# A clearing of an unread tile behind each gather in a two-layer graph network

## The chip, the cores and the metric

The kernel runs on one core of one Trainium2 chip. A core has five engines that work side by side, each in its own order: TensorE (PE; its weight loads are shown as PEld), VectorE (DVE), ScalarE (ACT), GpSimd (POOL) and SyncE (SP). They wait for each other through semaphores. Data moves between HBM and the on-chip memory SBUF through 16 DMA engines. Most transfers are issued by SP. Gathers, which fetch rows by a list of indices, are issued by GpSimd[...]. The metric is the device time of one execution in microseconds.

## The reference, cut to what matters

There are N = 3327 nodes with D = 256 features and an adjacency matrix of 3327 x 3327 whose entries are nonzero with a chance of 0.0024, plus the diagonal. So a row of it has about 9 nonzero entries.

```
h = relu(layernorm(x))
Xf = Xa = h;  Z = 0
R = (adj + I) / rowsum(adj + I)
for n in 0, 1:
    A  = top_p_attention(Xa, W1, W2, W3)   # softmax rows, cut to the largest that hold 0.9
    Xf = R @ Xf
    Xa = A @ Xa
    Z += Xf @ U1[n].T + Xa @ U2[n].T
x = x + layernorm(h + Z) * ln_g + ln_b     # layer 0
h = relu(layernorm(x))
d = (rowsum(adj) + 1e-9) ** -0.5
out = x + relu((d * adj * d) @ h @ W.T + b)   # layer 1
```

The attention is dense in its logits (3327 x 3327). The products with R and with the scaled adjacency are sparse. All numbers are float32.

## The kernel before, in words

The nodes are cut into 26 blocks of 128 rows (`NB`). The work is in stages that overlap at their edges. A start normalizes the nodes and makes keys, queries and products with weights. In stage 1 each block of the first attention step (`block_0`) runs beside `listing`, which finds the nonzero blocks of the adjacency, and `products_0`, the first sparse product. In stage 2 each block of the second attention step (`block_1`) runs beside `products_1`, the second sparse product. The last stage is the sparse product of layer 1 with its output product: 10 blocks of it (`DENSE`) as dense products over all of the adjacency's columns (`dense_product`, L1636), 16 by gathered rows.

**A sparse product by gathers.** For 128 rows, `listing` makes 8 slots (`SLOTS`) of 128 indices each. `gather_adj` (L759) fetches for one slot 128 pieces of adjacency rows into the tile `ac`; 8 of them make a block, and the result is stored to HBM (`ac_hbm`) and loaded again where it is needed. `gather_node` (L773) fetches for one slot 128 rows of 256 values (of `gb_hbm` in stage 1, `y_hbm` in stage 2, `hn_hbm` in the last stage) into a tile `vg`. `adj_gathered` (L783) multiplies the two on TensorE and sums over the 8 slots. There are 16 tiles `vg`, handed round in a list (`nodes_free`): a gather into one waits until TensorE has read it for the product before. In all there are 208 gathers of `ac` and 208 + 208 + 128 of `vg`, 752 together; in stage 1 a block has 16, in stage 2 and in a gathered block of the last stage 8. GpSimd's only other regular work is one addition per block in stage 2 (`add_bet`, L1349).

**What else runs beside them.** An attention block has logits on TensorE (L947), exponentials (L964) and passes over the whole row on ScalarE (L1008), a window pass (`window`, L1130) and a pass that drops what isn't kept (`drop_rest`, L1195) on VectorE, with small sorting steps between, turns of the weights on TensorE (L1209), copies by ScalarE (L1215) and the sum over values (`attend_sum`, L1224). The window and drop passes read 128x3327 values through two inputs in SBUF.

**What sets the order.** The order is written out by hand-kept numbers. `PLACES` names every step of each kind of block with a time; `BASES`, `PERIODS` and `SHIFTS` place the blocks, `MOVED` has blocks of their own, `EVENTS` single steps. `Plan` sorts all steps by these numbers and issues them one after the other. Each engine then does its share of them in that order, as soon as its waits are over; the numbers set no times beyond that.

Of the kernel before, what the change touches and what calls it, by code (L numbers as in the profile page):

```python
# [55 lines left out]
CODE = 4096  # L56
OFFSET = 4000.0
# [48 lines left out]
BASES = (-1.219, 871.121, -13.308, 19.608, 850.942, -80.36, 1724.847, 1716.49)  # L106
PERIODS = (30.0457, 29.9102, 30.2729, 28.5772, 29.0439, 1.6, 11.4283, 31.0222)
# [11 lines left out]
        ldq=-54.13, lg0=-39.852, ex0=-35.489, lg1=-29.838, ex1=-21.663, guess0=-20.859, guess1=-19.422,  # L119
        guess2=-19.336, guess3=-18.872, guess4=-18.507, guess5=-18.37, guess6=-15.915, ev1r=-13.296, ev1s=-9.29,  # L120
        st10=-8.997, st11=-5.99, guess7=-4.744, guess8=-3.502, st12=-3.403, st13=-3.094, st14=-1.343, st15=-1.159,
        st16=-0.991, st17=0.794, st18=1.518, win=9.292, wm2=9.574, wm1=9.968, wm3=12.534, wm0=12.544, sort0=13.403,
        cut0=14.026, sort1=14.125, sort2=14.543, sort3=16.481, sort4=17.004, sort5=17.559, sort6=17.939,
        sort7=18.592, thr=18.602, sort8=20.105, sort9=20.115, cut1=22.238, cut2=22.369, cut3=23.418, cut4=23.885,
        cut5=25.085, drop=25.681, inv=29.153, tr0=30.66, atc0=31.107, tr2=33.099, atc2=33.099, cut6=34.08,
        tr1=36.246, att0=36.894, atc1=37.192, tr3=40.273, atc3=41.533, att1=41.65, tr5=43.272, att2=44.935,
        att3=45.175, atc5=46.936, tr4=47.048, atc4=47.748, tr6=48.232, att4=52.752, atc6=54.181, att5=54.906,
        att6=58.725, attend=59.33, xtk_t=61.309, xtk_c=61.351, k_m=63.572, k_c=64.152, q_c=64.162, xu_m=66.376,
        xu_c=67.443, stxt=67.497, edge=70.682, stxu=75.618, stq=110.443,
    ),  # L130
    dict(
        ldq=-84.641, lg0=-64.92, ex0=-46.665, lg1=-45.76, ex1=-42.611, guess0=-42.569, guess1=-42.249,
        guess2=-42.014, guess3=-40.793, guess4=-40.513, guess5=-40.41, guess6=-40.216, ev1r=-34.894, ev1s=-32.942,
        mass0=-31.704, mass1=-31.672, mass2=-28.358, tail0=-26.851, tail1=-26.741, tail2=-26.526, tail3=-25.436,
        st10=-25.416, st11=-24.309, half=-23.772, aux0=-23.184, st12=-22.188, ev2s=-22.046, st13=-19.038,
        aux2=-18.425, thr=-17.708, st14=-16.622, btw1=-16.127, aux1=-13.861, sec10=-9.799, sec11=-7.489, sec12=-5.93,
        sec13=-5.256, nt2=-2.764, win=6.431, wm3=8.61, wm2=9.266, wm1=9.617, wm0=9.627, sort0=10.242, sort1=10.835,
        sort2=11.685, sort3=11.777, cut0=11.935, sort4=11.985, sort5=13.173, sort6=14.573, sort7=16.994,
        sort8=17.581, sort9=18.189, cut1=18.77, cut2=20.296, cut3=22.388, cut4=24.395, cut5=25.055, match=26.793,
        drop=27.95, tr0=29.85, tr1=31.048, atc0=31.434, tr2=32.44, atc1=32.946, edge=33.058, inv=33.905, att0=34.774,  # L140
        att1=34.905, atc2=35.47, tr4=35.49, tr3=36.814, att2=37.708, atc3=38.537, tr6=38.857, atc4=39.087,
        tr5=40.433, att3=40.469, atc6=45.474, atc5=46.334, att4=47.311, att5=47.868, att6=48.525, ldh=55.755,
        resid0=58.172, resid1=59.911, resid2=65.149, ldx=66.891, input20=69.622, root1=70.415, xbet=71.254,
        input21=73.884, input22=77.99, input23=79.538, root2=80.212, node2=88.781, stn=116.191,
    ),
    dict(
        lda1=-111.852, lda0=-108.627, flag1=-106.679, lda2=-105.584, flag0=-103.568, lda3=-101.391, flag2=-91.791,
        flag3=-91.183, listA0=-90.203, listA1=-87.679, listA2=-86.532, listA3=-82.435, listA4=-81.321,
        listA5=-78.466, listA6=-77.573, listN=-77.097, listA7=-76.714, listA8=-74.027, before=-70.418,
        beforec=-69.957, owners0=-68.346, owners1=-67.51, owners2=-63.593, shared=-56.741, lentc=-55.686,  # L150
        rows0=-50.814, rows1=-50.724, rows2=-47.7, rows3=-47.197, rows4=-42.132, rows5=-41.699, rows6=-41.116,
        rows7=-40.982, ga2=-14.404, ga0=-9.852, ga3=-4.385, ga4=-3.687, ga5=-2.371, ga1=-1.471, ga6=-0.85,
        ga7=-0.422, store=6.48,
    ),
    dict(
        gv4=5.839, gv2=20.97, gv1=22.589, gv6=25.502, lda=34.921, gv5=39.836, gv3=42.6, gv0=50.085, adj0=53.225,
        adj1=54.857, gv7=55.367, adj2=57.006, ldg=57.925, adj3=58.421, adj4=60.115, adj5=60.458, adj6=64.105,
        adj7=65.535, prop=68.632, roots=69.135, mixy=79.312, stxf=80.78,
    ),
    dict(  # L160
        gv4=8.024, gv2=8.104, gv0=13.177, ldt=16.082, gv3=17.924, gv6=25.033, gv7=28.341, lda=28.341, gv1=28.38,
        gv5=28.405, mix0=31.627, ld2=32.167, adj0=32.509, adj1=32.918, adj2=33.108, adj3=33.284, adj4=33.367,
        adj5=33.829, adj6=34.626, adj7=35.6, prop=44.561, scale=48.985, resid0=50.228, sthz=58.643,
    ),
    dict(
        mom=-13.994, node=-0.02, turn=0.915, turnc=2.784, proj=4.77, qc=7.477, stq=8.657, kc=9.12, gb=9.864,
        gc=10.785, stg=12.8, sth=161.359,
    ),
    dict(
        load=-27.7, gath=-6.539, prod=6.899, m=11.709, turn=14.704, mt=15.242, ldx=18.62, out=22.03, add=23.58,  # L170
        st=32.732,
    ),
    dict(
        row=-138.454, first=-124.233, second=-66.949, m=-52.332, ldx=-43.509, turn=-31.128, mt=41.499, out=99.246,
        add=109.349, st=109.933,
# [5 lines left out]
        12.63, 15.58, 13.76, 9.52, 14.85, 12.16, 7.33, 10.92, 12.38, 9.62, 10.05, 9.11, 6.13, 3.87, 5.9, 4.83, 5.04,  # L181
        3.38, -0.12, -0.81, -1.16, 0.73, -0.82, -1.47, -2.43, -4.06,
    ),
    (
        -3.42, -2.88, -2.0, -4.0, -2.87, -3.95, -4.64, -4.98, -5.17, -5.79, -6.06, -7.02, -7.66, -7.46, -7.61, -7.57,
        -8.28, -7.59, -8.88, -8.46, -8.36, -8.16, -9.1, -8.01, -8.45, -5.21,
    ),
    (
        48.05, 45.26, 47.07, 44.35, 35.7, 41.0, 31.58, 32.35, 22.91, 21.61, 15.75, 22.72, 14.28, 11.86, 11.76, 7.75,
        16.82, 22.71, 18.19, 32.24, 28.12, 25.64, 29.93, 25.27, 39.31, 42.78,  # L190
    ),
    (
        1.89, 8.61, 12.55, 21.95, 15.88, 24.02, 9.78, 15.75, 7.52, 3.91, 1.26, 4.72, 27.1, 31.73, 24.74, 37.8, 36.46,
        33.98, 33.66, 26.09, 37.71, 39.86, 24.21, 40.27, 31.79, 24.39,
    ),
    (
        -0.19, 2.55, 4.61, 10.25, 4.67, 3.99, 4.78, 7.69, 5.45, 6.63, 18.14, 12.33, 6.62, 6.28, 18.49, 11.75, 18.86,
        15.25, 8.72, 17.78, 22.41, 20.1, 23.47, 16.81, 9.48, 50.95,
# [5 lines left out]
        ldq=-53.671, lg0=-40.889, ex0=-37.137, lg1=-36.052, ex1=-32.766, guess0=-32.08, guess1=-32.08,  # L204
        guess2=-26.639, guess3=-26.046, guess4=-23.558, guess5=-23.104, guess6=-19.495, ev1s=-19.05, ev1r=-16.237,
        st10=-14.643, st11=-9.001, st12=-8.515, st13=-7.998, guess7=-6.427, st14=-6.323, guess8=-2.775, st15=-1.334,
        thr=-0.993, st16=0.358, st17=0.452, st18=4.273, win=4.393, wm0=7.365, cut0=7.398, wm3=8.486, wm2=8.644,
        wm1=9.137, sort0=9.72, sort1=10.861, sort2=12.3, sort3=12.31, sort4=15.195, sort5=15.397, sort6=15.646,
        sort7=16.912, sort8=17.349, sort9=18.279, cut1=20.61, cut2=20.899, cut3=22.232, cut4=22.242, cut5=23.179,
        drop=23.189, tr1=24.549, atc1=26.309, tr0=27.037, tr6=27.22, atc0=28.666, tr3=32.131, att0=32.131,  # L210
        att1=32.207, atc6=33.868, tr2=34.238, atc2=35.068, att2=35.264, atc3=38.695, tr4=41.024, tr5=48.015,
        atc5=49.222, att3=50.742, atc4=50.911, att4=50.919, att5=51.122, inv=51.9, att6=56.244, attend=57.45,
        xtk_t=58.899, xtk_c=60.185, k_m=66.789, edge=67.629, q_c=68.534, k_c=72.714, xu_m=75.139, stxt=85.201,
        xu_c=87.454, stq=93.482, cut6=93.886, stxu=100.697,
    ),
    (0, 1): dict(
        ldq=-96.445, lg0=-49.921, ex0=-34.349, lg1=-32.938, ex1=-28.697, guess0=-25.972, guess1=-25.962,
# [91 lines left out]
        adj4=-5.716, adj5=5.842, adj6=12.279, adj7=23.93, prop=24.426, scale=30.347, resid0=39.4, sthz=45.469,  # L309
    ),  # L310
    (6, 1): dict(
        load=-130.829, gath=-4.41,
    ),
    (6, 2): dict(
        gath=-14.181, load=3.453,
# [1554 lines left out]
```

## Time and profile before

Three runs took 1693.52, 1696.96 and 1696.99 us.

| | |
|---|---|
| Time of the runs, median | 1696.96 us |
| Profiled execution, its own time | 1863.65 us |
| Its span in the profile | 1861.8 us |
| Mean granted clock of TensorE in it | 0.94 |
| Gathers of `ac`, L759 | 208, 265.4 us busy, mean 1276 ns |
| Gathers of `vg` from `gb_hbm`, L773 | 208, 244.3 us busy, mean 1175 ns |
| Gathers of `vg` from `y_hbm`, L773 | 208, 301.6 us busy, mean 1450 ns |
| Gathers of `vg` from `hn_hbm`, L773 | 128, 121.3 us busy, mean 948 ns |
| First and last start of a gather in stage 1 | 101.6 and 908.7 us |
| First and last start of a gather in the last stage | 1629.2 and 1832.0 us |

The profiled execution took 9.8% longer than the runs, so its durations are those of that execution. Idle time is put down to what ended it. "Issue" is time in which an engine waited for nothing that the profile shows. "Remote" or "another core or an unknown queue" is a wait whose end the profile can't name; on one core that is a transfer or an instruction without a record. Some of TensorE's records are missing.[...]

### The profile page before, as it was taken

Reading aid. Unit: us, or ns where it says so; the run is one execution under the profiler, and the core shown is the slowest. Engines: PE = TensorE matmul, PEld = TensorE weight load, DVE = VectorE, ACT = ScalarE, POOL = GpSimd, SP = SyncE. Lnnn points to the kernel's source line nnn. Section 1 sums busy time; section 2 is a strip of 40 time slices with the busy share of each in tenths; the row PEclk is TensorE's granted clock in tenths of the full one; section 3 lists DMA queues with packets and bytes.
Section 4 is the critical chain, followed back from the end, with each engine's and each line's share of the span. In section 5 each row is a group of like instructions: output and inputs, shape, how many; then the busy total and the mean of one; then the engine's idle time right before and its main releaser. Section 6 shows DMA issues by size and latency. Waiting matters only on the chain.

```text
span 1861.8 us, 25048 instructions
## 1 busy us (share of the span) xinstructions
PE 1555.0 (84%) x7444; PEld 1202.7 (65%) x7444; DVE 1316.8 (71%) x3963; ACT 1147.3 (62%) x2694; POOL 964.7 (52%) x792
## 2 busy tenths in 40 slices
PE   5947788697899888888848989999989988988887
PEld 3526566475677565666636767777767767777676
DVE  5488678676898876766278899999989999601112
ACT  3566476465778665654387989998979986200000
POOL 0067467665677555754345345454555553065652
PEclk9959789898999898989979999999999999999999
DMA  6556656555555544543533333333334334356752
GB/s 188 170 161 190 191 151 183 175 167 161 152 181 179 175 144 132 176 135 109 159 95 91 107 108 111 113 115 95 114 107 135 92 117 147 114 201 216 240 171 88
DMA packets 148400, 272.54 MB, mean 146 GB/s; under 512 B 29347, under 2 KB 94240, under 8 KB 146976
## 3 DMA queue, kind: packets, MB, share of 16 engines
q1 hardware_dynamic: 109456, 183.94, 30.5%
q0 software_dynamic: 32768, 84.98, 16.2%
q10 hardware_dynamic: 6032, 1.93, 0.4%
q8 instruction: 61, 1.00, 0.2%
q14 instruction: 83, 0.68, 0.1%
HBM read 221.34 MB, written 49.41 MB: 145 GB/s over the span
## 4 chain that ended last, share of the span: by engine, by line
PE 46%; ACT 21%; DVE 14%; issue 8%; another core or an unknown queue 7%; DMA 2%; ACTq 0%; SPq 0%; DVEq 0%
PE att_acc L1224 16%; ACT ja L1008 8%; PE adj_acc L783 6%; PE p_t L1209 5%; PE p_l L947 5%; PE late_sums L1636 4%; ACT e L964 4%; ACT at L1215 3%; DVE cand L1137 3%; PE p_gb L857 2%; DVE w L1190 2%; PE late_acc L783 2%; DVE e L1195 2%; PE p_turn L807 1%
## 5 line engine op out<-in xcount | busy, mean ns | idle before, releaser
L1008 ACT ACTIVATE ja<-e,t 128x3327 uint8<-128x3327 f32 x127 | 389.6, 3068 | 1.7
L773 POOL DMA_INDIRECT vg<-y_hbm,v_idx x208 | 301.6, 1450 | 171.1 <-PE adj_acc L783 79.5
L759 POOL DMA_INDIRECT ac<-in_adj_t,a_idx x208 | 265.4, 1276 | 209.4 <-DVE crowd L697 89.0
L1224 PE MATMUL att_acc<-h,at 128*128 128x256 f32 (+1 forms) x1352 | 337.5, 397 | 35.3 <-ACT at L1215 34.8
L773 POOL DMA_INDIRECT vg<-gb_hbm,v_idx x208 | 244.3, 1175 | 178.0 <-PE adj_acc L783 103.8
L1215 ACT COPY at<-p_t 128x512 f32<-128x512 f32 (+1 forms) x364 | 193.9, 546 | 230.3 <-remote 82.1
L1224 PE MATMUL att_acc<-xa,at 128*128 128x256 f32 (+1 forms) x1352 | 325.0, 389 | 11.9 <-ACT at L1215 8.4
L1224 PEld LDWEIGHTS att_acc<-h,at 128*128 128x128 f32 (+1 forms) x1352 | 262.5, 200 | 80.8 <-ACT at L1215 38.7
L1224 PEld LDWEIGHTS att_acc<-xa,at 128*128 128x128 f32 (+1 forms) x1352 | 256.1, 195 | 50.4 <-ACT at L1215 12.6
L1209 PE MATMUL p_t<-ident,e 128*128 128x128 f32 x1352 | 208.2, 285 | 89.5 <-ACT at L1215 30.5
L1209 PEld LDWEIGHTS p_t<-ident,e 128*128 128x128 f32 x1352 | 162.7, 146 | 146.5 <-ACT at L1215 40.8
L783 PE MATMUL adj_acc<-vg,ac 128*128 128x257 f32 (+1 forms) x832 | 228.4, 398 | 15.2 <-DMA vg<-y_hbm,v_idx 7.3
L1137 DVE MAX8 cand<-w 128x8 f32<-128x208 f32 x832 | 238.3, 360 | 0.9
L947 PE MATMUL p_l<-kt,q 64*128 64x512 f32 (+1 forms) x832 | 191.1, 576 | 39.3 <-ACT e L964 33.8
L1130 DVE SCALAR_TENSOR_TENSOR w<-e,t 128x3327 f32<-128x3327 f32 x52 | 191.3, 3678 | 12.7 <-ACT u L978 4.7
L783 PEld LDWEIGHTS adj_acc<-vg,ac 128*128 128x128 f32 x832 | 154.6, 197 | 47.0 <-issue 10.1
L964 ACT ACTIVATE e<-p_l 128x2048 f32<-128x2048 f32 x104 | 161.6, 1554 | 28.6 <-PE p_l L947 8.0
L773 POOL DMA_INDIRECT vg<-hn_hbm,v_idx x128 | 121.3, 948 | 90.2 <-PE late_acc L783 54.1
L947 PEld LDWEIGHTS p_l<-kt,q 64*128 64x128 f32 x832 | 77.1, 198 | 128.6 <-issue 80.8
L1349 POOL TENSOR_TENSOR x_in<-x_in,bet 128x256 f32<-128x256 f32 x26 | 30.1, 1159 | 208.9 <-DMA x_in<-in_x 169.7
L811 ACT COPY xt_k<-p_turn 128x256 f32<-128x256 f32 x52 | 19.3, 373 | 161.4 <-PE p_turn L807 69.4
L651 DVE TENSOR_REDUCE most<-adj_sb 128x7 f32<-128x896 f32 x104 | 104.2, 1012 | 17.7 <-DMA adj_sb<-in_adj_t 7.9
(397 smaller groups left out, 2219.2 us busy)
## 6 DMA issues: line engine op xcount, KB each, us to landing
adj_sb<-in_adj_t SPq DMA_DIRECT2D x78, 448.0 KB
ac<-ac_hbm SPq DMA_DIRECT2D x68, 512.0 KB
adj_row<-in_adj_t SPq DMA_DIRECT2D x10, 1664.0 KB
ac_hbm<-ac SPq DMA_DIRECT2D x26, 512.0 KB
adj_sb<-in_adj_t SPq DMA_DIRECT2D x26, 320.0 KB
gb_hbm<-gb SPq DMA_DIRECT2D x26, 256.0 KB
gb<-gb_hbm SPq DMA_DIRECT2D x26, 256.0 KB
q<-q_hbm SPq DMA_DIRECT2D x104, 32.0 KB
```

The costliest lines, as they stand in the source:

```text
L651: nc.vector.tensor_reduce(s["most"][:, b0 : b0 + nb], s["chunk"].pop(c)[:, :nb, :], AX.X, ALU.max, apply_absolute_value=True)
L759: nc.gpsimd.indirect_dma_start(s["list"][:, k, :], None, adj_rows, bass.IndirectOffsetOnAxis(ap=s["a_idx"][:, k : k + 1], axis=0))
L773: nc.gpsimd.indirect_dma_start(t[:, :D], None, hbm[:, :], bass.IndirectOffsetOnAxis(ap=v_idx[:, i, k : k + 1], axis=0))
L783: nc.tensor.matmul(s["acc"][:, :width], s["ac"][:, k, :], rows[:, :width], start=(k == 0), stop=(k == SLOTS - 1))
L947: nc.tensor.matmul(pl[:, at : at + cw], s["q"][rows, :], kt[rows, c0 + c : c0 + c + cw], start=True, stop=True)
L964: nc.scalar.activation(halves(s["e"])[:, :, c0 : c0 + w], logits_of(s.pop(("l", g)))[:, :, :w], AF.Exp, accum_out=s["zp"][:, g : g + 1],)
L1008: nc.scalar.activation(junk, s["e"][:, :N], f, bias=s["t"], scale=-1.0, accum_out=s[name])
L1130: nc.vector.scalar_tensor_tensor(w[:, :N], ev, s["t"], ev, op0=ALU.is_le, op1=ALU.mult, accum_out=s["below"])
L1137: nc.vector.max(s["cand"][:, 8 * n : 8 * n + 8], s["w"][:, c0 : c0 + cw])
L1209: nc.tensor.transpose(pt[:, c : c + P], s["e"][:, b * P : (b + 1) * P], ident)
L1215: nc.scalar.copy(at[:, :w], pt[:, :w])
L1224: nc.tensor.matmul(s["att"][:, :D], at[:kb, c : c + P], v[b][:kb, :D], start=(b == 0), stop=(b == NB - 1))
```

## The change

Behind each gather, in `gather_adj` and in `gather_node`, GpSimd clears a tile `pace` of 128 x 576 float32 values. Nothing reads that tile. `BASES`, `PERIODS`, `PLACES`, `SHIFTS`, `MOVED` and `EVENTS` have new numbers throughout, and so every engine's order is a new one. The program has the same instructions as before apart from the 752 clearings. The lines of the new file stand 1 to 11 further down.

```diff
+PACE = 576
...
-BASES = (-1.219, 871.121, -13.308, 19.608, 850.942, -80.36, 1724.847, 1716.49)
-PERIODS = (30.0457, 29.9102, 30.2729, 28.5772, 29.0439, 1.6, 11.4283, 31.0222)
+BASES = (-1.195, 870.965, -13.311, 19.642, 853.079, -80.36, 1724.577, 1718.463)
+PERIODS = (30.0441, 29.9154, 30.273, 28.5719, 28.9512, 1.6, 11.802, 30.9401)
...
-        ga7=-0.422, store=6.48,
+        ga7=-0.66, store=9.794,
...
-        gv4=5.839, gv2=20.97, gv1=22.589, gv6=25.502, lda=34.921, gv5=39.836, gv3=42.6, gv0=50.085, adj0=53.225,
-        adj1=54.857, gv7=55.367, adj2=57.006, ldg=57.925, adj3=58.421, adj4=60.115, adj5=60.458, adj6=64.105,
-        adj7=65.535, prop=68.632, roots=69.135, mixy=79.312, stxf=80.78,
+        gv4=5.632, gv2=20.714, gv1=22.346, gv6=25.618, gv5=40.164, gv3=42.721, lda=44.817, gv0=50.312, adj0=52.657,
+        ldg=53.654, adj1=53.856, gv7=55.447, adj2=55.715, adj3=57.708, adj4=59.865, adj5=63.091, adj6=63.222,
+        adj7=64.567, roots=65.776, prop=68.869, mixy=74.572, stxf=96.762,
...
-        load=-27.7, gath=-6.539, prod=6.899, m=11.709, turn=14.704, mt=15.242, ldx=18.62, out=22.03, add=23.58,
-        st=32.732,
+        load=-23.985, ldx=0.485, gath=6.212, prod=12.722, m=19.141, turn=23.257, mt=24.311, out=26.194, add=31.048,
+        st=35.891,
...
-    keys=-30.497, centre=773.083, nodes=801.366, hn=830.787, last_nodes=902.39, roots=904.614, hn_last=1508.035,
+    keys=-30.531, centre=763.84, nodes=824.78, last_nodes=899.443, hn=928.418, roots=969.659, hn_last=1378.645,
...
     node_space = const.tile([P, 2 * SLOTS, D + 1], F32, name="vg")
+    pace = const.tile([P, PACE], F32, name="pace")
+
+    def paced():
+
+        nc.gpsimd.memset(pace, 0.0)
+
...
         nc.gpsimd.indirect_dma_start(
             s["list"][:, k, :], None, adj_rows, bass.IndirectOffsetOnAxis(ap=s["a_idx"][:, k : k + 1], axis=0)
         )
+        paced()
...
         nc.gpsimd.indirect_dma_start(
             t[:, :D], None, hbm[:, :], bass.IndirectOffsetOnAxis(ap=v_idx[:, i, k : k + 1], axis=0)
         )
+        paced()
```

## The prediction

> **What bounds the kernel now.** I read first the page's shares, then the stretches of the three stages, then GpSimd's (POOL's) own timeline. The page's first part says that no engine is full on average:
>
> ```profile
> PE 1555.0 (84%) x7444; PEld 1202.7 (65%) x7444; DVE 1316.8 (71%) x3963; ACT 1147.3 (62%) x2694; POOL 964.7 (52%) x792
> ```
>
> The 52% understates POOL. The busy times by stretch, with the stages cut where the gathers start and end (columns: stretch; its length; busy us of PE, PE's weight loads, VectorE, ScalarE, POOL; TensorE clock; DMA share; GB/s), and below them four blocks of stage 1 that ran almost undisturbed:
>
> ```profile
> 101.00:911.00 810.00, 658.09 (x3179) 503.98 (x3176) 602.01 (x1937) 488.97 (x1213) 510.42 (x417) 0.91 0.53 161
> 950.00:1610.00 660.00, 585.95 (x2895) 459.94 (x2896) 616.28 (x1720) 564.46 (x1233) 330.29 (x232) 0.97 0.37 112
> 1629.00:1841.00 212.00, 184.56 (x833) 156.69 (x833) 27.61 (x66) 10.48 (x30) 121.32 (x128) 0.97 0.60 197
> ...
> 543.60:648.40 104.80, 92.22 (x464) 70.62 (x463) 89.13 (x288) 74.83 (x184) 70.33 (x55) 0.96 0.57 179
> ```
>
> Stage 1 is bound by PE with stalls, stage 2 by VectorE (93%), the last stage by PE. In stage 1 a block takes 30 us on average by the starts of its window pass (L1130), 26.2 in those four (543.6 to 648.4). POOL's timeline there shows what its busy time leaves out: 0.30 us before each gather, and long gathers:
>
> ```profile
> 510.42 0.94 POOL L759 DMA_INDIRECT ac<-in_adj_t,a_idx  x1 [0.30 <-issue]
> 511.67 3.22 POOL L759 DMA_INDIRECT ac<-in_adj_t,a_idx  x1 [0.30 <-issue]
> 515.20 0.94 POOL L759 DMA_INDIRECT ac<-in_adj_t,a_idx  x1 [0.30 <-issue]
> ```
>
> VectorE's timeline has the reason, the drop pass from 510.38 to 514.08; the long gather ends 0.8 us after it:
>
> ```profile
> 510.38 3.70 DVE L1195 SCALAR_TENSOR_TENSOR e<-e,kept 128x3327 f32<-128x3327 f32 x1
> ```
>
> So one gather costs POOL 0.945 + 0.30 = 1.245 us, and a window or drop pass (two per block) holds it up for about 2.7 us more. In the four blocks POOL is taken for 70.3 + 55 x 0.30 = 86.8 of 104.8 us: 4.5 us per block are free. And PE already waits for POOL at times. The chain of waits around 440 us:
>
> ```profile
> 440.04 0.47 ACT at L1215
> 440.51 10.07 another core or an unknown queue
> 450.58 0.57 ACT at L1215
> ```
>
> In these 10 us POOL ends a run of 14 gathers with nothing between them (430.45 to 447.6), and PE resumes at about 450: I read it as PE standing at a product of gathered rows (L783) until the last of them had landed, with everything behind it in PE's order, the turns that ScalarE waits for among it.
>
> [...]
>
> **The change part by part.** *The clearing.* One 128x576 memset behind each of 208 + 208 + 208 + 128 = 752 gathers. Its size is not in the trace; the two nearest rows are
>
> ```profile
> masks.py:197 POOL MEMSET ident<- 128x128 f32 x1 | 0.2, 204 | 0.3 <-POOLq L1859 0.3
> L1859 POOL MEMSET const-float32-0.0<- 128x1 f32 x1 | 0.1, 98 | 0.2 <-issue 0.2
> ```
>
> (204 - 98)/127 = 0.83 ns per element, so 98 + 575 x 0.83 = 0.58 us; with the other one-column rows (up to 118 ns) it is 0.51.[...] I take 0.55. The gaps come from the only other work between gathers, the add L1349:
>
> ```profile
> 966.34 4.21 POOL L773 DMA_INDIRECT vg<-y_hbm,v_idx  x1 [0.30 <-issue]
> 970.57 0.73 POOL L1349 TENSOR_TENSOR x_in<-x_in,bet 128x256 f32<-128x256 f32 x1
> 971.46 0.97 POOL L773 DMA_INDIRECT vg<-y_hbm,v_idx  x1 [0.16 <-issue]
> ```
>
> The add follows the gather after 0.02 us, the next gather the add after 0.16, and lasts 0.97. So a paced gather takes 0.02 + 0.55 + 0.15 + 0.97 = 1.69 us in place of 1.245: +0.44. Ends: +0.25 if clearing and gap overlap, +0.60 if the gap stays 0.30 and the clearing is 0.58. In all 752 x 0.44 = 331 us of POOL time. The clearing waits only for the clearing before it, long done; queued behind it is the next gather, and for that PE's product.
>
> *Stage 1.* 416 gathers x 1.69 = 703 us, plus holds: now 509.7 - 416 x 0.945 = 117 us; a denser POOL meets each of the 52 passes, 52 x (3.68 - 1.69/2) = 147. Demand 820 to 850 us in a stretch of 810 that now has 810 - 510 - 125 (gaps) = 175 us free. That free time doesn't go to zero, since POOL works in order and waits for freed row tiles (104 us on PE adj_acc) and indices (23 us); as PE then waits for POOL, these shrink. I keep a third, 58 us: 835 + 58 - 810 = +83 us.
>
> *Stage 2.* 8 gathers per block, 208 x 0.44 = 92 us, and 330 + 208 x 0.30 = 392 of 660 taken now: 484 of 660. VectorE at 93% covers it: 0. Uncovered, the eighth gather of a block is 3.5 us late, at most 15 us over the stage where PE stood on it.
>
> *Last stage.* First to last gather 1629.2 to 1832.0 = 203 us; 127 x 1.69 = 215: +12, and of the 44 us that it waits now (54 us on late_acc by the waits) some stays: +18.
>
> *The order.* Against the old order, no gather moves by more than one place among POOL's gathers. Stage 1's gathered products move on average 0.4 places earlier in PE's order, by at most 22; so they get no more lead. Only in the last stage are they 11 places later on average and dense products as much earlier, which the +18 (not +26) takes in. SP's stores of y come 5 places later, its loads of gb 3 earlier, in a queue that mostly waits for VectorE; VectorE's edge step and ScalarE's thr, some 0.2 us each, move most. I put all that at 0, at most 10 us either way: a moved step that is late stalls PE as at 440.
>
> Sum: 83 + 0 + 18 + 0 = 101 us on the profiled 1861.8 (1863.65 with what lies around it). The timed runs are 165 us shorter, by what the trace can't say. If all stages shrink alike, stage 1 is 740 us and a demand of 835 overruns it by more; if gathers themselves are quicker there, by less. I keep about +98: 1697 + 98 = 1795.
>
> **The rivals.** *Hidden.* In timed runs a gather is much cheaper than 1.245 us; at 0.9, stage 1 demands 416 x 1.34 + 147 = 705 of 740 and the last stage is free: about +15, 1712. For it: the missing 165 us, much of which is PE stalled on gathers. Against: the four good blocks had 4.5 us free and get 16 x 0.44 = 7.0. *Saturated.* Pitch as in the profile and a stage of 740: 835 + 58 - 740 = +153, last stage +26: 1876. *Faster.* The new order of the last stage: PE idles there 212 - 184.6 = 27 us, mostly at gathered rows that are late; with dense products first all of it could go: 1670. It decides only if stage 1's clearings are free, that is for a gather under 26.2/16 - 0.44 - 5.7/16 = 0.84 us. That spacing itself helps speaks against the trace: rows land no later after long runs of gathers than after lone ones (the medians are near 2 us in both). *Nothing.* The clearing can't be left out: it is an instruction of its own.
>
> **How the numbers follow.** Slower by the sum or towards saturation 0.66 (own range 1740 to 1885); hidden 0.16; faster 0.14; within 0.2%, about what a measurement can tell from no change, 0.04. So faster 0.14, same 0.04, slower 0.82. The range drops most of the faster case and the top of the saturated one: 1690 to 1880.
>
> **What would show it.** Clearings of 0.5 to 0.6 us; 0.15 us before the gather behind each; POOL over 85% taken in stage 1; PE's waits on an unknown queue longer, its clock below 0.91 there; stage 2 unchanged. Wrong if the gaps swallow the clearing, or if stage 1 keeps 30 us a block.

## The result, and the profile after

The changed kernel takes **1881.67 us** (median of four runs, 1879.86 to 1882.07). The kernel before takes 1696.97 us beside it. The ratio is 1.109, with an interval of 1.107 to 1.111: the change costs 185 us. The forecast was 1795 us, with a range of 1690 to 1880.

One fact is needed to read every number below. In the experiments the kernel before takes 1695 to 1697 us on two chips, one set of runs on each, and 1865 to 1869 us on two others, one of which was used twice. I call them chips I and chips II. That it is the chip, and not something else that differed from one set to the next, is not shown beyond these five sets. Chips I are compared with chips I and chips II with chips II, unless the text says otherwise. By its times the result is of chips I, and the profile ahead of the prediction, at 1864 us, of chips II. The first experiment, a repeat of the kernel before on a chip I, has the profile to lay beside the profile after.

The first part of the page, in the kernel before on a chip I, and after:

```profile
PE 1508.6 (89%) x7444; PEld 1178.1 (69%) x7444; DVE 1316.4 (78%) x3963; ACT 1145.9 (67%) x2694; POOL 995.1 (59%) x792
```

```profile
PE 1566.1 (83%) x7444; PEld 1205.4 (64%) x7444; DVE 1335.4 (71%) x3963; ACT 1141.7 (61%) x2694; POOL 1381.4 (73%) x1544
```

POOL went from 995 us to 1381 us of busy time. TensorE, at a granted clock of 0.93 in place of 0.97, went from 1509 to 1566; the other two kept theirs. POOL's row of the 40 slices (busy tenths) shows where, first in the kernel before on a chip I:

```profile
POOL 0047658888888868886273554355565653166762
```

and after:

```profile
POOL 0059999999999999899958855665865584289994
```

Stage 1 (slices 3 to 20) is 9 nearly throughout, and so is the last stage but for its ends. Stage 2 between them is not. By stretch (columns as in the prediction; the first stretch after ends 42 us past the last gather of stage 1), after:

```profile
101.00:1000.00 899.00, 698.80 (x3329) 534.56 (x3326) 653.55 (x2019) 536.57 (x1326) 795.86 (x854) 0.88 0.50 153
1000.00:1640.00 640.00, 593.24 (x2986) 466.80 (x2986) 600.87 (x1685) 548.54 (x1213) 390.00 (x427) 0.99 0.39 120
1640.00:1880.00 240.00, 200.17 (x852) 162.28 (x850) 32.42 (x78) 12.33 (x36) 193.62 (x251) 0.91 0.52 168
```

and the kernel before on a chip I:

```profile
102.00:798.00 696.00, 626.51 (x3194) 490.17 (x3192) 600.50 (x1935) 488.17 (x1214) 536.22 (x416) 0.96 0.61 187
798.00:1493.00 695.00, 618.07 (x3073) 482.80 (x3070) 632.97 (x1755) 596.17 (x1311) 335.49 (x236) 0.97 0.39 118
1493.00:1698.00 205.00, 190.11 (x889) 162.36 (x887) 32.37 (x78) 12.62 (x36) 121.45 (x128) 0.99 0.63 208
```

TensorE's clock fell from 0.96 to 0.88 in stage 1 (0.89 over its gathers alone, 107 to 958 us) and from 0.99 to 0.91 in the last stage, the two in which it now idles longer: 177 of 851 us over those gathers in place of 69 of 696, and 40 of 240 in place of 15 of 205. Whether the idle time lowers the clock was not tested. Two groups of the page, in the kernel before on a chip I (busy us, mean ns, idle us before it and what ended most of that):

```profile
L773 POOL DMA_INDIRECT vg<-gb_hbm,v_idx x208 | 278.5, 1339 | 78.1 <-issue 42.2
L783 PE MATMUL adj_acc<-vg,ac 128*128 128x257 f32 (+1 forms) x832 | 222.7, 390 | 9.3 <-DMA vg<-y_hbm,v_idx 6.7
```

and after:

```profile
L631 POOL MEMSET pace<- 128x576 f32 x752 | 447.6, 595 | 0.4
L768 POOL DMA_INDIRECT ac<-in_adj_t,a_idx x208 | 274.5, 1320 | 130.4 <-DVE a_idx L757 96.4
L794 PE MATMUL adj_acc<-vg,ac 128*128 128x257 f32 (+1 forms) x832 | 229.0, 402 | 88.5 <-DMA vg<-gb_hbm,v_idx 43.8
L783 POOL DMA_INDIRECT vg<-gb_hbm,v_idx x208 | 255.9, 1230 | 38.5 <-issue 27.8
```

A clearing takes 595 ns and waits for nothing (0.4 us ahead of all 752). The idle time ahead of the gathers from `gb_hbm` was 78 us, of which 23 us came from waiting for row tiles that TensorE still had to read. Now 38.5 us are left, mostly the gap that each has, and the waits for row tiles are 1 us. The dependence has turned round: TensorE stands 88.5 us ahead of L794, half of it for rows of `gb_hbm`, where it stood 9 us ahead of L783 and not for those. POOL's timeline in stage 1:

```profile
498.93 2.95 POOL L768 DMA_INDIRECT ac<-in_adj_t,a_idx  x1 [0.17 <-issue]
501.88 0.60 POOL L631 MEMSET pace<- 128x576 f32 x1
502.64 0.95 POOL L783 DMA_INDIRECT vg<-gb_hbm,v_idx  x1 [0.17 <-issue]
503.59 0.59 POOL L631 MEMSET pace<- 128x576 f32 x1
504.35 0.95 POOL L768 DMA_INDIRECT ac<-in_adj_t,a_idx  x1 [0.16 <-issue]
```

The clearing starts when the gather ends, and the next gather 0.165 us after the clearing. So a gather takes 0.95 + 0.595 + 0.165 = 1.71 us, where it took 1.245. The stage has 416 of them, 711 us. Their time above 0.945 us, the holds under VectorE's passes (2.95 us in the first line is one), adds up to 137 us; the 52 of them that take over 1.2 us each meet such a pass. The sum is 848 us. From the first gather to the last, stage 1 takes 851: POOL has nothing free.

### The profile page after: what moved, and what is told of

Same layout as the page of the kernel before. It is cut to its first block, busy times and chain, and to the rows that moved or that the text cites. A ratio compares the mean times of both kernels' runs of the same rounds, so it can differ in the third digit from the quotient of the medians.

```text
span 1879.8 us, 25790 instructions
## 1 busy us (share of the span) xinstructions
PE 1566.1 (83%) x7444; PEld 1205.4 (64%) x7444; DVE 1335.4 (71%) x3963; ACT 1141.7 (61%) x2694; POOL 1381.4 (73%) x1544
## 5 line engine op out<-in xcount | busy, mean ns | idle before, releaser
L631 POOL MEMSET pace<- 128x576 f32 x752 | 447.6, 595 | 0.4
L768 POOL DMA_INDIRECT ac<-in_adj_t,a_idx x208 | 274.5, 1320 | 130.4 <-DVE a_idx L757 96.4
L1235 PE MATMUL att_acc<-xa,at 128*128 128x256 f32 (+1 forms) x1352 | 317.1, 381 | 0.8 <-ACT at L1226 0.8
L794 PE MATMUL adj_acc<-vg,ac 128*128 128x257 f32 (+1 forms) x832 | 229.0, 402 | 88.5 <-DMA vg<-gb_hbm,v_idx 43.8
L783 POOL DMA_INDIRECT vg<-y_hbm,v_idx x208 | 251.3, 1208 | 63.3 <-issue 30.0
L783 POOL DMA_INDIRECT vg<-gb_hbm,v_idx x208 | 255.9, 1230 | 38.5 <-issue 27.8
L1235 PEld LDWEIGHTS att_acc<-xa,at 128*128 128x128 f32 (+1 forms) x1352 | 248.8, 191 | 33.0 <-ACT at L1226 1.8
L794 PEld LDWEIGHTS adj_acc<-vg,ac 128*128 128x128 f32 x832 | 156.5, 199 | 123.6 <-DMA vg<-gb_hbm,v_idx 47.0
L958 PE MATMUL p_l<-kt,q 64*128 64x512 f32 (+1 forms) x832 | 186.8, 569 | 40.2 <-ACT e L975 37.2
L783 POOL DMA_INDIRECT vg<-hn_hbm,v_idx x128 | 122.3, 955 | 42.7 <-DMA hn_hbm<-hn_last 18.9
```

The source lines that it names most:

```text
L631: nc.gpsimd.memset(pace, 0.0)
L768: nc.gpsimd.indirect_dma_start(s["list"][:, k, :], None, adj_rows, bass.IndirectOffsetOnAxis(ap=s["a_idx"][:, k : k + 1], axis=0))
L783: nc.gpsimd.indirect_dma_start(t[:, :D], None, hbm[:, :], bass.IndirectOffsetOnAxis(ap=v_idx[:, i, k : k + 1], axis=0))
L794: nc.tensor.matmul(s["acc"][:, :width], s["ac"][:, k, :], rows[:, :width], start=(k == 0), stop=(k == SLOTS - 1))
L958: nc.tensor.matmul(pl[:, at : at + cw], s["q"][rows, :], kt[rows, c0 + c : c0 + c + cw], start=True, stop=True)
L1235: nc.tensor.matmul(s["att"][:, :D], at[:kb, c : c + P], v[b][:kb, :D], start=(b == 0), stop=(b == NB - 1))
```

## The experiments

**Lengths between gathers.** Every experiment is read by three lengths in its trace: stage 1 (first to last of its 416 gathers), stage 2 (from there to the first gather of the last stage) and the last stage (first to last of its 128 gathers). All times in us; "pitch" is what a gather takes with its gap and clearing.

| Kernel | chip | runs' median | pitch | stage 1 | stage 2 | last |
|---|---|---|---|---|---|---|
| before | I | 1695.5 | 1.245 | 695 | 695 | 176 |
| new order, no clearing | I | 1734.7 | 1.245 | 738 | 681 | 182 |
| new order, clearing of 16 | I | 1738.8 | 1.245 | 736 | 682 | 189 |
| old order, 216 | I | 1735.7 | 1.405 | 730 | 691 | 183 |
| old order, 576 at half the gathers | I | 1771.2 | 1.48 | 757 | 694 | 189 |
| old order, 576 | I | 1894.9 | 1.71 | 851 | 696 | 220 |
| changed kernel | I | 1881.7 | 1.71 | 851 | 677 | 220 |
| before (first profile) | II | 1865 to 1869 | 1.245 | 807 | 721 | 203 |
| new order, no clearing (profile of the longest run, 2041) | II | 2023.2 | 1.245 | 923 | 766 | 216 |
| old order, 144 | II | 1857.2 | 1.34 | 807 | 722 | 203 |
| old order, 288 | II | 1774.7 | 1.47 | 759 | 694 | 192 |
| new order, 288 | II | 1783.0 and 1781.6 | 1.47 | 773, 775 | 681, 678 | 199, 192 |
| old order, 576 in stage 1 only | II | 1900.7 and 1904.0 | 1.71 there | 850 (2nd) | 710 | 206 |
| old order, 576 in stage 2 only | II | 1862.1 | 1.71 there | 815 | 706 | 207 |
| old order, 576 in the last stage only | II | 1874.2 and 1877.0 | 1.71 there | 803 (2nd) | 727 | 221 |
| changed kernel | II | 1883.7 | 1.71 | 849 | 679 | 221 |

In the expectations of the first runs, theory A is that POOL is full in stage 1 and in the last stage, so that its demand sets their lengths; each names its rival. From the thirteenth run on, A and B are the two theories on the stalls of chips II.

### The kernel before again, the order alone, the clearing alone, a short clearing

The first is unchanged. The second takes the clearings out of the changed kernel:

```diff
-        paced()
...
-            paced()
```

The third puts them into the kernel before, whose order it keeps:

```diff
+        paced()
...
+        paced()
```

The fourth is the changed kernel with

```diff
-PACE = 576
+PACE = 16
```

> The kernel before, unchanged, with a new profile. The profile shown of it took 1864 us where its runs took 1697. Theory A (GpSimd's pace sets stage 1): the runs repeat 1697, and if this profiled execution also takes about 1697, its gathers stand at a shorter distance than the 1.245 us of the first profile, or its waits behind them are gone. Rival B (the first profile is what the kernel is like, the runs are a special case): the runs spread between 1697 and 1864.

> The new order without the clearings. Theory A: the clearings are the cause, the new order is worth little: 1680 to 1720 us. Rival O (the new order itself costs): 1800 us or more. If the order gains anything at all, it shows here as less than 1690.

> The old order with all 752 clearings of 576 values. Theory A: about the same as the changed kernel, 1860 to 1910 us, since the new order gives gathers no more lead in stage 1. Rival O: near 1700, as the old order hides them.

> The changed kernel with a clearing of 16 values in place of 576, still 752 of them. A clearing of 16 columns took 0.12 us in the trace of before, and the gap ahead of a gather behind another instruction was 0.15 in place of 0.30, so a gather with it takes 0.02 + 0.12 + 0.15 + 0.97 = 1.26 us, as much as one without. Theory A (the length of what stands between gathers counts): 1690 to 1730 us. Rival S (each further instruction and its wait costs, whatever its length): 1800 or more.

Measured, as ratios to the kernel before: 0.999 (0.998 to 1.001), 1.023 (1.019 to 1.026), 1.117 (1.114 to 1.121) and 1.025 (1.022 to 1.028). The clearing alone makes the whole loss and 13 us more. The new order alone costs 38 us, which I had put at nothing; by it the second and the fourth also lie above the ranges of theory A. The new order is 43 us longer in stage 1, 14 us shorter in stage 2. In the changed kernel the longer stage 1 is hidden, since POOL's 848 us are more than either order's stage 1 without clearings (both take 851 us with them), and the shorter stage 2 stays: this is how the changed kernel comes out below the clearing alone. Why the new order lengthens stage 1 by itself these runs do not say.

The fourth takes 4 us more than the second: 752 more instructions are not the cost, their length is. POOL's timeline with the 16-value clearing:

```profile
499.54 0.95 POOL L783 DMA_INDIRECT vg<-gb_hbm,v_idx  x1 [0.18 <-issue]
500.49 0.12 POOL L631 MEMSET pace<- 128x16 f32 x1
500.79 0.95 POOL L783 DMA_INDIRECT vg<-gb_hbm,v_idx  x1 [0.18 <-issue]
```

A gather still follows the last by 1.25 us: the clearing of 0.12 us stands in the gap of 0.30 us that was there anyway.

### Clearings in one stage alone

All three keep the old order. The clearing stands in `gather_adj` and, under `if hbm is gb_hbm:`, in `gather_node` for stage 1, and under the same condition with `y_hbm` or `hn_hbm` alone for the other two. These ran on a chip II, where I had expected I.

```diff
+        if hbm is hn_hbm:
+            paced()
```

> The old order, clearings behind the 416 gathers of stage 1 only (adjacency pieces, and rows of gb). Theory A (GpSimd is full in stage 1): with 1.71 us per gather and the measured holds, GpSimd needs 416 x 1.71 + 138 = 849 us there instead of 695, so 1847 us. Rival D (the clearings cost wherever they stand, in proportion to their number): 416 of 752 of the 198 us, 1806 us.

> The old order, clearings behind the 208 gathers of rows of y in stage 2 only. Theory A: VectorE sets this stage and GpSimd has room: 1695 to 1705 us. Rival D: 208 of 752 of the 198 us, 1752 us.

> The old order, clearings behind the 128 gathers of the last stage only. Theory A: 128 x 1.71 = 219 us in place of the 176 that these gathers take, so 1735 to 1745 us. Rival D: 128 of 752 of the 198 us, 1731 us; the three runs together tell A from D, this one alone does not. Rival L (the last stage waits for TensorE and for rows of the adjacency): below 1710.

Ratios: 1.016 (1.011 to 1.022), 0.996 (0.994 to 0.999) and 1.004 (1.002 to 1.006). Those in stage 2 cost nothing, as theory A had it; in the clearing alone on a chip I, too, stage 2 keeps its length, 696 us for 695. The other two cost 34 and 7 us, far below what theory A wanted. But the kernel before had taken 1867 us there, and in the table the stages *without* clearings of these kernels are long: 206 and 207 us for the last stage, where chips I have 176. A fourth kernel, without clearings and with the new numbers for stage 2 and the last stage alone, was expected at 1680 to 1690 us. After its last stage it took the general path, which the kernel runs when a count at its end finds something lost, so its 9890 us say nothing. Its stages before that took 797, 766 and 214 us. On this chip II the new numbers make stage 2 45 us longer than the old (766 also in the new order alone, in the table), where on a chip I they make it 14 us shorter.

A repeat of two, with the changed kernel and one of half the width (`PACE = 288`):

> The changed kernel, order and all, with the clearing at half its width (288 values a row; the same 752 of them). Theory A (a full GpSimd: nothing is lost until its own demand in a stage passes the stage's length without it): a clearing of 0.36 us makes a pitch of 0.945 + 0.36 + 0.165 = 1.47 us; stage 1 then wants 416 x 1.47 + 140 us of holds = 752 us from first to last gather, where the 16-value clearing took 736; the last stage wants 127 x 1.47 = 187 us, where it took 189. So about +18 us on the 16-value clearing, some 1757 us (1745 to 1775), on a chip where before takes about 1697; well short of half of the full clearing's 142 us. Rival B (each clearing delays its product by its own length, whatever GpSimd has free): half way between the 16-value and the full clearing, (1739 + 1882)/2 = 1810 us. On a chip where before takes about 1865, stage 1 is 807 us long without clearings and A expects 1870 or so.

> The old order with clearings behind the 416 gathers of stage 1 alone. On a chip where before takes about 1697, theory A (full GpSimd): stage 1's gathers stretch from 695 to 416 x 1.71 + 137 = 848 us, +153, so about 1845 us (1830 to 1865), and the last stage keeps its 176 us. Rival B (the free time in stage 1 is that of the first profile, about 175 us, of which two thirds can be used): +34 us as on the other chip, about 1735. On a chip where before takes about 1865: a repeat of +34 us.

> The old order with clearings behind the 128 gathers of the last stage alone. On a chip where before takes about 1697, theory A: the gathers of that stage stretch from 176 to 127 x 1.71 + 3 = 220 us, +44, of which about 40 at the end: some 1737 us (1725 to 1745). Rival B (the stage is bound by TensorE and the clearing hides, as it all but did on the other chip at +7): 1700 to 1710.

> The changed kernel unaltered. On a chip where before takes about 1697: 1880 us again. On a chip where before takes about 1865: theory A (a GpSimd that is full sets its time, and GpSimd's durations are the same on both chips) expects little more than on the faster one, 1880 to 1910 us, a change of +1 to +2% in place of +11%; rival B (the slower chip adds its 165 us whatever bounds the kernel) expects some 2045 us.

It was chips II again: 0.954 (0.948 to 0.959), 1.020 (1.014 to 1.026), 1.004 (1.002 to 1.006) and 1.009 (1.005 to 1.012). The changed kernel takes 1884 us, 2 us more than on chips I. And with 288 values it takes 1783, **86 us less** than the kernel before on that chip, where theory A had expected 1870. Both say that what stalls the kernel before on chips II costs these two kernels little or nothing.

### What stalls on chips II

The first profile has them. The prediction read 10 us at 440 us as TensorE waiting for gathered rows. VectorE's timeline just ahead of it:

```profile
437.75 0.28 DVE L1150 MATCH_REPLACE8 cand<-val,cand 128x128 f32<-128x128 f32 x1
439.04 0.29 DVE L1147 MAX8 val<-cand 128x8 f32<-128x128 f32 x1 [1.01 <-DVE cand L1150]
...
439.71 0.28 DVE L1150 MATCH_REPLACE8 cand<-val,cand 128x128 f32<-128x128 f32 x1
441.17 0.29 DVE L1147 MAX8 val<-cand 128x8 f32<-128x128 f32 x1 [1.19 <-DVE cand L1150]
```

Here VectorE waits over 1 us for its *own* last instruction. The kernel before on a chip I, at the same step:

```profile
399.09 0.28 DVE L1150 MATCH_REPLACE8 cand<-val,cand 128x128 f32<-128x128 f32 x1
399.40 0.29 DVE L1147 MAX8 val<-cand 128x8 f32<-128x128 f32 x1
```

There it goes on after 0.03 us. TensorE and ScalarE in the first profile:

```profile
439.50 0.66 PE L1209 MATMUL p_t<-ident,e 128*128 128x128 f32 x4
439.94 0.57 ACT L1215 COPY at<-p_t 128x512 f32<-128x512 f32 x1
450.56 0.58 ACT L1215 COPY at<-p_t 128x512 f32<-128x512 f32 x1 [10.05 <-remote]
```

and ScalarE on a chip I:

```profile
402.00 1.06 ACT L1215 COPY at<-p_t 128x512 f32<-128x512 f32 x2
```

The second copy takes turns of TensorE that had ended at 440.16 (four from 439.50, 0.66 us); on a chip I the two copies follow each other, done 1.06 us after the first began. No gathered row is in that wait, and "remote" is here no instruction without a record: the turns have theirs, and the signal that ends the wait comes at 450.54. What is late is the hand-over, from an engine to another (10 us here) or to itself (1.0 and 1.2 us above).

This pair of instructions on VectorE gives a measure. It comes 134 times in the old order and 111 times in the new one, in stages 1 and 2. On chips I, in all kernels, every one of these hand-overs takes 34 to 36 ns. In the first profile 8 of the 134 take over 0.2 us, up to 2.5 us. They all lie in stage 1, and each of them where five gathers or more had been issued in the 6.5 us before (so had 34 of the stage's 62 hand-overs; of the other 28 none was late). In the kernels on chips II that keep the old order and leave stage 1 without clearings there are 6 to 9 of them, mostly near the same places (208 to 216, 409 to 415 and 435 to 443 us in all four). In those with 288 or 576 values there, none.

The semaphore records of the traces give a second measure: how long after the end of a TensorE instruction its signal comes, for the signals that an instruction waited for and started within 0.1 us of. In the seven profiles of chips I none comes more than 0.03 us after. In stage 1 of the first profile 56 of 182 come over 0.2 us after, up to 9.6 us, 114 us in all; in its stage 2 it is 12 signals, in its last stage 14. On chips II the three kernels with clearings of 576 in one stage have none in that stage and keep them in the others, and the changed kernel has none anywhere. A clearing of 288 values thins them but does not remove them: in stage 1 of the old order 37 of 183 are still late, up to 3.2 us, 38 us in all, and 30 and 32 in the two profiles of the new one. The old order with 288 values shows both measures side by side:

```profile
664.44 0.28 DVE L1159 MATCH_REPLACE8 cand<-val,cand 128x128 f32<-128x128 f32 x1
664.75 0.29 DVE L1156 MAX8 val<-cand 128x8 f32<-128x128 f32 x1
665.82 0.44 PE L1218 MATMUL p_t<-ident,e 128*128 128x128 f32 x2 [0.17 <-issue]
667.89 0.59 ACT L1224 COPY at<-p_t 128x512 f32<-128x512 f32 x1 [2.13 <-remote]
```

VectorE goes on after 0.03 us; ScalarE's copy starts 1.6 us after the last turn, which ended at 666.26.

### The order or the spacing, and how much of it

> The new order without clearings, so gathers follow each other at 1.245 us. On a chip where before takes about 1867: theory A (hand-overs between instructions come late there while gathers are packed at 1.245 us, whatever the order) expects the stalls to stay: 1735 + 165 = about 1900 us (1860 to 1930), and single hand-overs of over 1 us on VectorE in stage 1. Theory B (the stalls come of the old order) expects about 1735 us, as on the other chip, and none of them. On a chip where before takes about 1697: 1735 us again.

> The old order with a clearing of 144 values a row behind each gather: about 0.23 us, so a pitch of 0.945 + 0.23 + 0.165 = 1.34 us in place of 1.245. Stage 1 wants 416 x 1.34 + 145 = 702 us, where it has 695 without stalls; the last stage 127 x 1.34 = 170 of 176. On a chip where before takes about 1867: theory A (packed gathers make hand-overs late) expects the stalls to shrink or go if 0.1 us more between gathers is enough: 1705 to 1740 us, some 8% faster than before; if it is not enough, 1850 and more. Theory B (the old order makes the stalls): 1867 or more. On a chip where before takes about 1697: 1705 us (1697 to 1720).

> The old order with a clearing of 288 values a row (0.356 us) behind each gather: pitch 1.47 us. Stage 1 wants 416 x 1.47 + 145 = 756 us where it has 695, the last stage 187 where it has 176. Theory A: no late hand-overs, so 1697 + 61 + 11 = about 1770 us on either chip. Theory B: on a chip where before takes about 1867 the stalls stay and this is 1870 to 1890 us; on the other 1770.

> The changed kernel with 288 values a row. 1783 us again on a chip where before takes about 1867. On a chip where before takes about 1697: 1745 to 1785 us (a full GpSimd alone makes 1757), against 1810 if each clearing delayed its product by its own length.

All on a chip II: 1.084 (1.077 to 1.092), 0.997 (0.994 to 0.999), 0.954 (0.948 to 0.960) and 0.958 (0.952 to 0.964). It is the clearings, and their length, not the order. The new order alone has late hand-overs too (4 of VectorE's 111, two of them in stage 2; 46 of TensorE's signals in stage 1, 172 us in all), and its 2023 us are worse than theory A's 1900: it stalls more than the old one. The old order with 0.36 us of clearing, nothing else changed, takes 1775 us where 1770 was expected: stage 1, at 759 us, is as long as a POOL at that pitch makes it, 416 x 1.47 + 149 = 761 us, and stage 2 takes the 694 us that it has on chips I. So the signals that are still late cost stage 1 nothing more; POOL's own time covers them. In the new order with 288 values stage 1 takes 773 and 775 us, 12 to 14 above the sum; whether the late signals or the order makes these was not separated. With 144 values hand-overs are still late (4 of VectorE's 134, up to 0.7 us; 51 of TensorE's signals in stage 1, up to 10 us), and stage 1 keeps its 807 us.

The last two were to find where between a pitch of 1.34 and 1.47 us the stalls stop costing, and whether it is the mean pitch that counts or each gap:

> The old order with a clearing of 216 values a row (about 0.295 us) behind each gather: pitch 1.405 us, between the 144 values that left the stalls (1857 us) and the 288 that took them away (1775 us). Theory A1 (the stalls go at some pitch below 1.40): stage 1 wants 416 x 1.405 + 147 = 731 us where 288 values made it 759; so about 1745 us (1730 to 1755) on a chip where before takes about 1867, the best of the sizes. Theory A2 (they shrink smoothly from 1.34 to 1.47): stalls of half their size remain and fill what is saved, 1790 to 1830 us. On a chip where before takes about 1697: 1735 us.

> The old order with the full clearing of 576 values, but only behind gathers of odd slots, so half of them: a mean pitch of (1.245 + 1.71)/2 = 1.48 us, that of 288 values behind each. If the mean rate of gathers makes the stalls, about 1775 us like 288 values behind each (1765 to 1790). If two or three gathers following each other at 1.245 us are enough, the stalls stay: 1840 us and more, with hand-overs of over 1 us on VectorE. On a chip where before takes about 1697: 1775 us either way.

They ran on a chip I, so both stay open: that the clearings act by spacing the gathers, and not in some other way, is argued from their length alone. What they show is the other half: 1.024 (1.021 to 1.026) and 1.045 (1.041 to 1.049), 1735.7 and 1771.2 us where 1735 and 1775 were expected, stage 1 at 730 and 757 us where the sum made 731 and 758. With chip II's 759 at 1.47 us and 851 at 1.71, the length of stage 1 follows pitch x 416 + holds to within 3 us at all four pitches above 1.4 of the old order. On chips I every clearing of 216 values or more that was run costs; on chips II the best that was run is the old order with 288 values, 4.6% faster than before, and no kernel here beats the kernel before on chips I.

## Why the prediction was wrong

**Right: the direction, and the price of a paced gather.** The 1.69 us came out at 1.71. The clearing is 0.595 us, a little above the upper end of 0.58; the gap 0.165. The forecast gave the clearings no holds under VectorE's two-input passes. That was the author's estimate, and the trace after has its numbers: 42 of the 752 clearings lie wholly under such a pass and take 595 ns on average (602 at most), as the others do; the longest of all takes 0.71 us. Of the 77 gathers that start under such a pass, six end before it does, after 0.95 us each; the other 71 take 2.77 to 4.41 us, and 70 of these end 0.80 to 0.83 us after the pass.

**Right: stage 1's demand.** 835 us (820 to 850) were forecast, 848 found, with holds of 137 us where 147 were worked out. (The "about 2.7 us" that a pass was said to hold up POOL did not fit the profile it was read from, where 117 us over 52 passes make 2.25; the changed kernel's 137 make 2.6.)

**Wrong: the length that the demand was held against.** "A stretch of 810 that now has 175 us free" is the step that failed. On chips I, to which the timed runs belong by their time, that stretch is 695 us, its demand 416 x 1.245 + 144 = 662, and 33 us are free. The 115 us between are in the profile of a chip II only. Late hand-overs are what the traces show there and not on chips I: TensorE's signals alone come 114 us late over stage 1. Which of them lie on the path that set the stage's length was not worked out, so that they make all of the 115 us is likely and not shown. The prediction had two signs of it. Its own four undisturbed blocks took 26.2 us each, as blocks do on chips I (26.1 by the starts of the window passes), where stage 1 averaged 30. And the timed runs were 165 us below the profile, "by what the trace can't say". It kept the base all the same.

**Wrong the other way: "I keep a third, 58 us"** of POOL's idle time. It kept 3 (851 against 848). The waits for freed tiles in stage 1, 23 us on a chip I before, are 1 us now that TensorE waits for POOL. So stage 1 came out at 851 - 695 = +156 us in place of +83: 115 from the base, 13 more from the demand (848 for 835), less 55 for idle time that did not stay.

**Right: stage 2 at 0.** Its length fell from 695 to 677 us by the new order (681 without clearings), and the clearings cost it nothing (696 us in the old order with all of them).

**Wrong by the same base: the last stage, +18.** First to last gather takes 220 us, as forecast (215 and some idle), but 176 before, not 203: +45 (220.4 for 175.7). On chips II, from 203 to 221, the change is the 18 us that were forecast.

**Wrong by itself, right in the sum: the order at 0.** It costs 38 us alone, and against a POOL that is full it gains 13 (1881.7 against 1894.9).

**Wrong: the reading of the 10 us at 440** as TensorE at a product of gathered rows. It was a late hand-over. With it falls the argument that spacing can't help because "rows land no later after long runs of gathers" (medians near 2 us there): landings were the wrong thing to look at. On chips II clearings do help, by 90 us at 288 values in the old order.

**The rivals.** *Saturated*, 1876 us, is what happened, though it hit the number in part by luck: its 740 us of stage 1 were still too long and its 58 us of idle time too many, and these cancel. *Hidden* is out: a gather takes the same 0.945 us on chips I and II. *Faster* did not come about on chips I. On chips II the price of the clearings and the stalls that go with them nearly cancel: 1.009.

By the pieces, from the starts of the window passes in the two profiles on chips I, the changed kernel is longer by 11 us until the first block of stage 1 (the new order alone adds 12 there), 132 over stage 1, 5 in the passage, -6 in stage 2 and 39 after the last block's window pass. That is 181.6 us, the difference of the spans.

## What to carry to other kernels

Before adding an engine's new work to a stretch, take the stretch's length from blocks that ran undisturbed, or from the timed runs, not from a profiled execution that is longer than these; idle time that exists only in a longer execution (175 us free in stage 1 of the profile, 33 in that of the timed runs) is no cover. Work out pitch x count + holds for an engine that issues gathers: its busy share (59% over the span here) hides that it is all but full in one stage, and from there on all that is added to each gather is paid in full (stage 1 here from a pitch of 1.4 us on). And when waits are long, look at hand-overs whose giver and taker are the same engine: if these are late (1.0 and 1.2 us at 440 us in the first profile, 0.03 us on a chip I), it is not data that is late. The reverse does not hold: with 288 values VectorE's own hand-overs are on time (0.03 us) while some of TensorE's signals come up to 3.2 us late.

## What the runs showed that I had not expected

- The same kernel differs by 10% from chip to chip (1697 against 1867 us), with the same time for a gather (0.945 us). On chips II VectorE's hand-overs to itself, 35 ns elsewhere, take 0.2 to 4.6 us at times while gathers follow each other at 1.245 or 1.34 us, and never in the stages with 1.47 us or more. TensorE's signals are late there too, by up to 9.6 us in the first profile; some still are at 1.47 us, and none in a stage at 1.71 us. Why the chips differ, and what delays a hand-over where gathers follow each other closely, was not settled.
- A clearing of 16 values behind each of the 752 gathers is all but free (4 us in all): it fits into the 0.30 us ahead of the next one, which shrinks to 0.18.
- A clearing takes 0.130, 0.235, 0.356 and 0.595 us at 16, 144, 288 and 576 values a row, 0.83 ns a value, the rate that the two small clearings in the first profile give.
